# Layer 0 of a four-layer image network: attention with queries on the partitions instead of keys, and layer 2's row sums 1024 wide

## The chip, the cores and the metric

The kernel runs on one core of a Trainium2 chip. The metric is device time in microseconds (us) from start to end of one execution.

## The reference

The input x is four images (samples) of 128 channels by 64 x 64 = 4096 pixels, f32. Four layers follow each other; the change lies in layer 0 and in a small part of layer 2. Layer 0 for one sample:

```python
q = (q_w @ x + q_b).reshape(C, n)          # C = 128, n = 4096
v = (v_w @ x + v_b).reshape(C, n)
w, b = two small nets on q                 # (n,) each
norm   = sqrt(sum(q * q, axis=0))
k      = q / clip(norm, 1e-4)
logits = einsum('cn,cm->nm', k, q)         # keys n, queries m
mean   = mean(logits, axis=0)
sparse = relu(logits - mean * w[None, :] + b[None, :])
attn   = softmax(logits * sparse, axis=0)  # over the keys
attn   = clip(attn * (sparse != 0), 1e-8)
out    = einsum('cn,nm->cm', v, attn)
y = leaky(conv3x3(out) + lin_b) + x
```

Layer 1 is a state-space scan over the pixels of each sample (64 states), layer 2 a softmax attention whose logits are products of one number per row and one per column, and layer 3 two state-space scans over all samples.

## The kernel before

All samples pass layers 0 and 1 in turn: `layer0(b)`, `layer1(b)`, for b = 0 to 3. Layer 2 of sample b - 1 is worked off beside the layers of sample b: its row sums in `row_weights(b - 1)`, whose `beside(i)` is called once in each iteration of layer 0 (samples 1 to 3), and its products in `attend` beside layer 1. Layer 3 ends the kernel.

All instructions of the stages are recorded by a helper (line 111) that keeps program order on each engine. So each engine does its own instructions in the order in which the Python code issues them, and a wait holds up all that stands behind it on that engine. Nearly all groups in the profile therefore have the line L111 and are told apart by the names of their tiles.

`layer0` keeps keys on the partitions. A chunk c is 512 queries (`NCH` = 8 chunks). Iteration i of its loop takes one chunk's 512 queries and 256 keys: U = 16 iterations a chunk, S = 128 a sample. The steps of a tile of 128 x 2 x 512:

- `logits(i)`: two f32 matmuls into `lg` (PSUM, two buffers of two banks);
- `above(i)`, VectorE: t = lg + ncut, with the threshold `ncut` a 128 x 512 tile that repeats the row on all partitions;
- `weights(i)`, VectorE: e = max(t, 0) * lg;
- `shifted(i)`: GpSimd subtracts `bound` (an upper bound of the exponent per query), ScalarE takes Exp; every second t gets its sign from ScalarE;
- `sums(i)`, every second iteration: 32 columns of ones by e, in four column groups, add up `zs`, the sum of a query's weights over its keys;
- `masked(i)`: t becomes e where t > 0, on GpSimd and VectorE in turn;
- `floored(i)`, VectorE: the floor of 1e-8 times the sum, `fl`, which exists only when all keys of a chunk are done. So it runs LAG = 18 iterations behind;
- `product(i)`: two matmuls of values `vT` by t into `acc`, one iteration later.

`scales(c)` turns the sum into a floor and a factor 1/Z, `image(c)` multiplies `acc` by it into the padded image `ypad` (VectorE), and `convolved(c)` does the 3 x 3 convolution (nine matmuls), Prelu and residual. `thresholds(c)` makes `ncut` and `bound` for a chunk with four wide matmuls. These smaller steps wait in a queue; each iteration takes at most two of them and then one that starts with TensorE. The loop runs on for LAG + 2 iterations after the last logits, and there `first_tokens` (the first steps of layer 1) join in.

In sample 0 a loop ahead of this makes q, its norm and the keys k; for the others `tokens(b + 1)` in layer 1 does so and stores q, k and the norms (as rows) in DRAM.

`row_weights` gives ScalarE two activations of 512 columns an iteration (`junk`), each with a sum over its columns.

## Time and profile before

| | |
|---|---|
| three runs, median (lowest to highest) | 10499.42 us (10498.93 to 10503.0) |
| profiled execution, first to last instruction | 10494.9 us |
| busy in it: TensorE, VectorE, ScalarE, GpSimd | 8443.5, 9159.8, 6387.1, 8156.1 us |
| layer 0, sample 0: first logits to first scan of layer 1 | 59.3 to 786.0 us |
| the same, sample 1 | 1681.6 to 2423.8 us |
| layers 1 of the four samples | 786 to 1645, 2424 to 3307, 4085 to 4966, 5742 to 6610 us |
| last layer 2, then layer 3 | 6610 to 6950, 6950 to 10495 us |

The profile gives the span of the instructions alone; the median of the runs lies 4.5 us above it. Times of stages come from the first and last instruction of a kind in the trace. In the groups below a line reads: line, engine, operation, tile written and tiles read, shape, count, then busy time, mean length in ns of one, and the engine's idle time just before them with what ended it. The granted clock (PEclk) is TensorE's, as a share of full speed.

### The profile page before, as it was taken

Reading aid. Unit: us, or ns where it says so; the run is one execution under the profiler, and the core shown is the slowest. Engines: PE = TensorE matmul, PEld = TensorE weight load, DVE = VectorE, ACT = ScalarE, POOL = GpSimd, SP = SyncE. Lnnn points to the kernel's source line nnn. Section 1 sums busy time; section 2 is a strip of 40 time slices with the busy share of each in tenths; the row PEclk is TensorE's granted clock in tenths of the full one; section 3 lists DMA queues with packets and bytes.
Section 4 is the critical chain, followed back from the end, with each engine's and each line's share of the span. In section 5 each row is a group of like instructions: output and inputs, shape, how many; then the busy total and the mean of one; then the engine's idle time right before and its main releaser. Section 6 shows DMA issues by size and latency. Waiting matters only on the chain. (4 is left out here: it accounts for less than half of the span.)

```text
span 10494.9 us, 91078 instructions
## 1 busy us (share of the span) xinstructions
PE 8443.5 (80%) x28013; PEld 3021.6 (29%) x28088; DVE 9159.8 (87%) x6318; ACT 6387.1 (61%) x9576; POOL 8156.1 (78%) x3574
## 2 busy tenths in 40 slices
PE   8996667997887997887898887877777777777775
PEld 3331213332223333223333222322222222222221
DVE  7869998887998886999886999359999999999996
ACT  3334545666665665666665776456666666677765
POOL 6758896766887775888674888149999999989986
PEclk9997788998998999998999999888988989888886
DMA  1018882007885005887102888158888888888896
GB/s 37 12 37 201 194 194 85 18 14 189 211 203 149 15 14 129 201 213 191 33 16 63 206 211 200 32 133 199 207 198 206 204 202 208 215 223 224 228 227 176
DMA packets 512313, 1552.75 MB, mean 148 GB/s; under 512 B 84017, under 2 KB 91825, under 8 KB 511825
## 3 DMA queue, kind: packets, MB, share of 16 engines
q1 hardware_dynamic: 511824, 1546.92, 58.9%
q8 instruction: 223, 3.65, 0.2%
q14 instruction: 266, 2.17, 0.1%
HBM read 1349.40 MB, written 137.48 MB: 142 GB/s over the span
## 5 line engine op out<-in xcount | busy, mean ns | idle before, releaser
L111 POOL TENSOR_TENSOR p<-h,c_rep 128x1024 f32<-128x1024 f32 x2048 | 4807.9, 2359 | 734.8 <-DVE h L111 673.7
L111 DVE TENSOR_TENSOR_SCAN h<-da,carry,db 128x1024 f32<-128x1024 f32 x1536 | 3603.4, 2346 | 200.5 <-ACT da L111 17.8
L111 PE MATMUL db<-parts,sel 96*128 96x512 bf16 x4096 | 1401.5, 428 | 1460.3 <-DVE h L111 1408.2
L111 ACT ACTIVATE da<-row,A 128x1024 f32<-128x1024 f32 x1536 | 1761.1, 1147 | 359.4 <-DMA row<-d 341.0
L111 DVE TENSOR_TENSOR db<-b_rep,db 128x1024 f32<-128x1024 f32 x1536 | 1853.5, 1207 | 112.1 <-PE db L111 92.0
L111 POOL TENSOR_TENSOR e<-e,bound 128x1024 f32<-128x1024 f32 x512 | 1241.3, 2427 | 573.5 <-DVE e L111 573.0
L111 POOL TENSOR_TENSOR x<-row,b_rep 128x1024 f32<-128x1024 f32 x512 | 1208.8, 2361 | 123.8 <-DMA row<-d 122.8
L111 DVE TENSOR_TENSOR_SCAN h<-db,carry,x 128x1024 f32<-128x1024 f32 x512 | 1194.9, 2334 | 62.9 <-ACT db L111 35.3
L111 PE MATMUL total<-p,gather 128*32 128x512 f32 x8192 | 1225.7, 719 | 9.8 <-POOL p L111 9.8
L111 ACT ACTIVATE db<-db,A 128x1024 f32<-128x1024 f32 x512 | 555.3, 1085 | 1080.6 <-PE db L111 1026.5
L111 ACT ACTIVATE e<-e 128x1024 f32<-128x1024 f32 x512 | 540.9, 1057 | 1051.9 <-POOL e L111 1051.8
L111 PEld LDWEIGHTS <-sel 96*128 96x128 bf16 x4096 | 309.6, 101 | 3002.0 <-DVE h L111 2017.3
L111 PE MATMUL lg<-q,k 128*128 128x512 f32 x2048 | 1021.5, 623 | 106.5 <-DVE e L111 98.3
L111 PE MATMUL acc<-t,vT 128*128 128x512 f32 x2048 | 964.1, 595 | 3.3 <-DVE t L111 3.3
L111 PE MATMUL acc<-e,values 128*128 128x512 f32 x1536 | 854.9, 648 | 88.8 <-ACT e L111 62.9
L111 DVE TENSOR_TENSOR t<-lg,ncut 128x1024 f32<-128x1024 f32 x512 | 624.5, 1220 | 288.1 <-PE acc L111 264.0
L111 ACT ACT_TABLE_LOAD x617 | 791.6, 1283 | 38.8 <-DMA r<-y 12.3
L111 ACT ACTIVATE e<-gq,below,fcol 128x512 f32<-128x512 f32 x768 | 610.2, 805 | 87.0 <-PE acc L111 86.7
L111 POOL TENSOR_TENSOR t<-t,e 128x1024 f32<-128x1024 f32 x256 | 610.4, 2384 | 45.4 <-ACT t L111 45.4
L111 ACT ACTIVATE junk<-gp,ntop,fcol 128x512 f32<-128x512 f32 x768 | 619.5, 807 | 30.4 <-DMA gp<-g 17.7
L111 ACT COPY carry<-h 128x1 f32<-128x1 f32 x2048 | 373.5, 185 | 416.4 <-DVE h L111 411.4
L111 DVE SCALAR_TENSOR_TENSOR e<-t,lg 128x1024 f32<-128x1024 f32 x512 | 618.5, 1208 | 1.2
(259 smaller groups left out, 9927.5 us busy)
## 6 DMA issues: line engine op xcount, KB each, us to landing
row<-d SPq DMA_DIRECT2D x2048, 512.0 KB
parts<-split SPq DMA_DIRECT2D x912, 64.0 KB
b_rep<-bc SPq DMA_DIRECT2D x96, 512.0 KB
c_rep<-bc SPq DMA_DIRECT2D x96, 512.0 KB
d<-delta SPq DMA_DIRECT2D x76, 384.0 KB
r<-y SPq DMA_DIRECT2D x48, 512.0 KB
xq<-in_x SPq DMA_DIRECT2D x72, 256.0 KB
res<-x SPq DMA_DIRECT2D x32, 512.0 KB
```

What stands on the lines that cost most here:

```text
L111: return self.tc.keep_in_program_order(method(*args, **kwargs))
```

## The change

Queries go on the partitions. A tile is now 128 queries by 1024 keys; four tiles (J = 4) hold all keys of 128 queries, and a chunk still has U = 16 iterations.

- Threshold and bound are now one number per partition (`ncut`, `nbound`, 128 x 4 a chunk). `above` is a Relu with bias on ScalarE (all tiles of sample 0, every second of the others) or an add and max on VectorE. `weights` multiplies r by lg.
- Exp takes `nbound` as its bias and adds up its row (`accum_out`), so GpSimd's subtraction and the `sums`, `fl`, `zt`, `rz` matmuls go. `signs` makes r the mask on GpSimd (on ScalarE for odd tiles of sample 0); `masked` is on GpSimd for all tiles.
- `scaled(g)` makes `diag`, the identity times 1/Z, once for four tiles.
- `turned(i)`: eight 128 x 128 matmuls, weights e, moving operand `diag`, put the scaled weights back with keys on the partitions (`pt`, PSUM, one buffer). `floored` is a max with 1e-8 into `w`. `product` does eight matmuls of 128 columns. LAG is 6.
- `image` is a copy on ScalarE, and stands behind the next `product` in the loop.
- The norms stay in SBUF (`own`, 128 x 32), so the norm rows in DRAM and the steps that make them in layer 1's `tokens` go (`turned(u)`, `kept(u)` and a store there, other steps than the new `turned(i)`).
- `row_weights` has one activation of 1024 columns an iteration instead of two of 512.

```diff
-        LAG = U + 2
+        LAG = 6
...
+                def columns():
+                    held["th"] = misc("col_ps")[:, 0 : 3 * A].rearrange("p (a t) -> p t a", t=3)
+                    for a in range(A):
+                        m = bass.ts(a, P)
+                        pe.matmul(held["th"][:, 0:2, a], held["h"][:, m], self.w2, start=True, stop=True)
+                        pe.matmul(held["th"][:, 2:3, a], qs[c][:, m], kbar, start=True, stop=True)
...
+            def above(i, on_act):
+                if i < S and bool(b == 0 or i % 2 == 0) == on_act:
+                    c, a, j = at(i)
+                    r[i] = rp.tile([P, 2, NB], F32, name="r", tag="r")
+                    if on_act:
+                        act.activation(r[i], lg[i], AF.Relu, bias=ncut[c][:, a : a + 1])
+                    else:
+                        dve.tensor_scalar(flat(r[i]), flat(lg[i]), ncut[c][:, a : a + 1], 0.0, ALU.add, ALU.max)
+            def weights(i):
+                e[i] = ep.tile([P, 2 * NB], F32, name="e", tag="e")
+                dve.tensor_tensor(e[i], flat(r[i]), flat(lg.pop(i)), ALU.mult)
+            def exped(i):
...
+                act.activation(
+                    e[i], e[i], AF.Exp, bias=nbound[c][:, a : a + 1], accum_out=z[i // J][:, j : j + 1],
+                )
+                if b == 0 and i % 2:
+                    act.activation(r[i], r[i], AF.Sign)
+            def signs(i):
+                if b or i % 2 == 0:
+                    t = flat(r[i])
+                    pool.tensor_scalar(t, t, 0.0, None, ALU.is_gt)
+            def masked(i):
+                pool.tensor_tensor(e[i], e[i], flat(r.pop(i)), ALU.mult)
+            def turned(i):
+                pt[i] = turned_pair()
+                t = e.pop(i)
+                for m in range(N):
+                    pe.matmul(
+                        flat(pt[i])[:, bass.ts(m, P)], t[:, bass.ts(m, P)], diag[i // J], start=True, stop=True,
+                    )
+            def floored(i):
+                w[i] = wp.tile([P, N, P], F32, name="w", tag="w")
+                dve.tensor_scalar(flat(w[i]), flat(pt.pop(i)), 1e-8, None, ALU.max)
+            def product(i):
+                c, a, j = at(i)
+                if a == j == 0:
+                    acc[c] = ps1.tile([P, NB], F32, name="acc", tag="acc")
+                for m in range(N):
+                    pe.matmul(
+                        acc[c][:, bass.ts(a, P)], vT[:, N * j + m, :], w[i][:, m, :],
+                        start=(j == 0 and m == 0), stop=(j == J - 1 and m == N - 1),
+                    )
+            def image(c):
+                act.copy(ypad[...], acc.pop(c)...)
...
+                o = i - LAG
                 if i < S:
                     weights(i)
+                if 0 <= o < S:
+                    turned(o)
+                if 0 <= o - 1 < S:
+                    product(o - 1)
+                    if (o - 1) % U == U - 1:
+                        due[i + 1] = (o - 1) // U
                 if i + 2 < S:
                     logits(i + 2)
+                above(i + 1, True)
+                beside(i)
+                if i < S:
+                    exped(i)
+                    signs(i)
+                if 0 < i <= S:
+                    masked(i - 1)
+                    if i % J == 0:
+                        scaled(i // J - 1)
+                if 0 <= o < S:
+                    floored(o)
+                above(i + 1, False)
                 if i in due:
                     d = due.pop(i)
                     image(d)
```

## Prediction

> **What bounds the kernel now.** I read the page first: the chain of waits is empty here (it covers the last DMA alone), so the shares by engine are only an average over stages. I then split the span into stages. Layer 0 runs four times, from the start or from the last scan of layer 1 before it: 0 to 786, 1647 to 2424, 3310 to 4085 and 4969 to 5742 us. The rest the change hardly touches. The sum of engine times in single chunks of 512 queries (from one write of `ypad` to the next) comes next:

> ```profile
> core 0: us, PE busy (x) PEld busy (x) DVE busy (x) ACT busy (x) POOL busy (x), PEclk, DMA share, GB/s
> 393.13:473.40 80.27, 80.19 (x239) 31.70 (x238) 70.14 (x64) 27.38 (x30) 59.54 (x27) 1.00 0.05 14
> 2021.25:2103.74 82.49, 79.81 (x237) 31.23 (x236) 71.77 (x62) 54.45 (x93) 58.75 (x27) 1.00 0.05 16
> ```

> One chunk takes 80.3 us in sample 0 and 82.5 us in the others; TensorE is busy for 80.2 and 79.8 us of it at the full granted clock. VectorE's 71 us are close behind but below. What TensorE does there, in the groups of the second window:

> ```profile
> L111 PE MATMUL lg<-q,k 128*128 128x512 f32 x65 | 31.5, 605 | 2.0 <-DVE e L111 2.0
> L111 PE MATMUL acc<-t,vT 128*128 128x512 f32 x64 | 30.1, 592 | 0.0
> L111 DVE TENSOR_TENSOR t<-lg,ncut 128x1024 f32<-128x1024 f32 x16 | 19.5, 1221 | 10.7 <-PE acc L111 10.7
> L111 PE MATMUL conv_ps<-ypad,lin_wT 128*128 128x512 f32 x18 | 9.0, 609 | 0.0
> L111 PE MATMUL zs<-e,ones 128*32 128x512 f32 x64 | 8.5, 605 | 0.0
> ```

> TensorE waits 2 us in 82 for VectorE; VectorE waits 10.7 us for TensorE. A mean of 592 ns is a latency, since matmuls are pipelined; the price of one is the distance between starts. TensorE's timeline gives it (start, span, engine, operation, count):

> ```profile
> 1689.37 1.05 PE L111 MATMUL v_ps<-v_wT,xq 128*128 128x128 f32 x8
> 1690.26 1.02 PE L111 MATMUL lg<-q,k 128*128 128x512 f32 x2
> ...
> 2343.74 3.60 PE L111 MATMUL conv_ps<-ypad,lin_wT 128*128 128x512 f32 x8
> 2347.17 1.02 PE L111 MATMUL lg<-t,W_in 128*128 128x512 f32 x2
> ...
> 2354.04 1.84 PE L111 MATMUL lg<-mean_c,t 128*128 128x1 f32 x16
> 2355.74 2.82 PE L111 MATMUL acc<-t,vT 128*128 128x512 f32 x6
> ```

> Every matmul of the program is two instructions here (the two logits of an iteration and sample half stand as x4 and 64 a chunk). One with 512 moving columns costs (2347.17 - 2343.74)/8 = 0.429 us; one with 128 columns and weights of its own 0.89/8 = 0.111 us; one with a single column and new weights 1.70/16 = 0.106 us, so below 128 columns the weights set the price. Check on a chunk: 128 x 0.429 for `lg` and `acc` = 54.9; `zs`, four column groups at once, 64 in 7.9; convolution 18 x 0.429 = 7.7; thresholds 3.9; `fl`, `zt`, `rz` 2.8: 77.2, and 79.8 were busy. The accounting holds to 3%.

> **TensorE, part by part.** An iteration keeps its area (128 queries by 1024 keys for 256 keys by 512 queries), so `lg` stays at 4 x 0.429 = 1.72 us.
> - Removed: `zs` 7.9, `fl`, `zt`, `rz` 2.8, three of the four wide threshold matmuls (2.9) a chunk: 13.6 us.
> - Added: `turned`, 8 matmuls by `diag`, 16 instructions of 128 columns with 16 weight loads: 16 x 0.111 = 1.79 us an iteration, 28.5 us a chunk. The 16 small `columns` instructions, 16 x 0.106 = 1.7 us.
> - Dearer: `product` has the same columns, but 16 x 0.111 for 4 x 0.429: 28.5 instead of 27.5.

> After: 27.5 + 28.5 + 28.5 + 7.7 + 1.0 + 1.7 = 94.9 us, against 77.2 by the same accounting. No arrangement of the other engines gets below that.

> [...] The rows above say 111 and 429 for these f32 instructions, and I go by them.

> **The other engines, per iteration of at least 5.3 us.** VectorE: `weights` 1.21 (one operand in PSUM, as `e<-t,lg`), `floored` 1.21 (as `t<-t,fl`), `above` 1.21 every second time: 3.0. ScalarE: `above` as Relu, between 1.06 (`e<-e`) and 1.24 (the 1024 wide Identity with a bias); Exp with sum the same plus the 0.19 read of the accumulator; the row sum at 1024 wide: 0.81 at 512 and 3.80 at 4096 give 1.23, plus 0.19. In samples 1 to 3 that is 0.62 + 1.42 + 1.42 = 3.5; in sample 0 1.23 + 1.42 + half a Sign 0.52 = 3.2. GpSimd: `masked` 2.36 as now; `signs` has no row, it lies between 1.6 (eight times the 0.20 of a 128 wide memset) and 2.36 (a two-operand pass): at most 4.7. All are below 5.3, so none of it is paid, and neither is what the wider row sums save (2 x 0.99 - 1.42 = 0.6 us an iteration of ScalarE, already hidden behind TensorE). [...]

> **Waits.** `turned` waits for three engines, and `product` and `logits` stand behind it: `floored` of the iteration before ended some 2 us earlier, `diag` two iterations and `masked` five earlier. `logits` wait for `weights`, done early in the iteration. One wait is new and real: `acc` has one buffer, and `product` of a new chunk now stands ahead of `image`, which ScalarE does behind Relu, row sum and Exp: 1.23 + 1.42 + 1.42 + 0.6 = 4.7 us, less the 1.8 of `turned`. It costs 0 to 3.2 us at seven chunk ends; I take 2.3, as ScalarE starts a little ahead: about 97 us a chunk. Weight loads may also show after a wait: `lg` behind `zs` takes 1.82 instead of 1.72, so up to 0.1 at each of two places an iteration. I take 0, since after a full-width group (`acc` behind `lg`, 2020.87 to 2022.59) it is not seen.

> **Ends of the stage.** Now: first `lg` to first scan is 59.3 to 786.0 = 726.7 us in sample 0 and 1681.6 to 2423.8 = 742.1 in the others (sample 1). After:
> - the six iterations before the first `turned`: TensorE has 23 us of work (8 x 1.72 logits, seven values at 0.9, one threshold 2.7), the chain logits 1.9, Relu, `weights`, then Exp behind the row sum in one ScalarE queue, up to 6 an iteration, 36; taken 33, nearer the chain, since nothing else runs yet;
> - 122 iterations, 7.6 chunks of 97.2 = 741, less the 1.6 convolutions that come later (12): 729;
> - the tail: 13 passes of 1.79 = 23, convolutions 6 and 7 15.5, the first tokens 10.6 of TensorE, now beside 6 iterations instead of 18, waits between them some 10, and as now 18.4 us from the last convolution to the scan (2405.4 to 2423.8): 77.

> That is 839 for samples 1 to 3; sample 0, without row sums in ScalarE's queue, gets 3 less: +97 three times and +109. Ahead of it, sample 0 loses the 1x512 norm matmuls, roots and stores (eight chunks of 4.66 us; -5, between 0 and -8). In the others the `norms` load, `kbar_rep` and two wide matmuls go, but `values(0)` is waited for first: +2 each. The two `norms` steps leave layer 1's tokens, which run beside scans: 0. Sum: 291 + 109 + 1 = +401. The profiled execution spans 10,494.9 us, so 10,896; the median of the three runs lies 4.5 above that span: **10,900 us**.

> **Rivals.**
> 1. TensorE binds as above: 10,900, between 10,740 (no wait at `acc`, -64; the first six iterations and the tail at TensorE's work alone, -96) and 11,000 (0.1 us at two places of 512 iterations, +102). Chance 0.83.
> 2. GpSimd binds. The point is `signs` above 97.2/16 - 2.36 = 3.7 us. At 4.7 (twice a two-operand pass) iterations of samples 1 to 3 take 7.1: +1.0 x 128 x 3 = 384, 11,280; at 4.0, 11,010. For: no row. Against: no operation of that width here takes over 2.45 on average. Chance 0.08.
> 3. TensorE's gate: a granted clock of 0.9 instead of 1.0 in layer 0 adds a tenth to 4 x 777 us of TensorE work (eight chunks, values, tokens): 11,210. Layer 1 runs at 0.76 to 0.92, but with idle gaps; the busiest chunks of layer 0 are at 1.00. Chance 0.04.
> 4. Faster: short matmuls overlap better in long runs than in the bursts of 8 and 16 seen here. It decides at 0.09 us: 7.6 x (38 + 512 x 0.09) + 98 = 738, about the 742 of now. [...] Against it: even one column takes 0.106. Chance 0.03.
> 5. The change hides wholly, as if TensorE had been waiting: within 0.2%, 10,500. The 0.1 us of idle in sample 0's chunk speaks against it. Chance 0.02.

> The range of 10,740 to 11,070 is rival 1's own with the milder half of rival 2. Faster by over 0.2% (about what a measurement of this kernel can tell from no change) 0.03, same 0.02, slower 0.95.

> **What would show it.** Right: in layer 0 a chunk takes 96 to 99 us, TensorE busy all but 3 of them, `pt` and `acc` 256 instructions a chunk each with 0.111 between starts; VectorE under 55 us a chunk, GpSimd under 80, waits of `acc` for `ypad` once a chunk; layers 1 and 3 as long as before. Wrong: distances of the 128 wide matmuls under 0.09 or over 0.13; a TensorE wait for GpSimd's `e` in each iteration; a clock under 0.97 in layer 0; a tail over 100 us.

## The result, and the profile after

The changed kernel takes **11,022.1 us** (median of four runs, 11,020.6 to 11,024.6) against 10,499.3: **1.0497 times** as long, 95% interval 1.0482 to 1.0512. The forecast was 10,900 in a range of 10,740 to 11,070. Direction, mechanism and range held, the range in part by luck (see below); of the 523 us, 401 were foreseen.

TensorE binds, as forecast. The chunks of layer 0 after, in the same columns as before (two of sample 0, two of sample 1, each from one write of `ypad` to the next):

```profile
409.40:509.50 100.10, 98.06 (x612) 76.76 (x612) 38.91 (x43) 46.30 (x66) 61.17 (x28) 0.98 0.03 9
509.50:611.20 101.70, 99.71 (x612) 78.09 (x612) 38.87 (x43) 46.24 (x66) 61.16 (x28) 0.97 0.03 9
2062.30:2164.30 102.00, 99.72 (x612) 77.90 (x612) 49.16 (x51) 49.97 (x82) 83.13 (x37) 0.97 0.05 14
2164.30:2264.70 100.40, 98.10 (x612) 76.07 (x612) 49.17 (x51) 49.97 (x82) 83.18 (x37) 0.98 0.03 9
```

A chunk takes 100 to 102 us (80.3 and 82.5 before, 96 to 99 forecast); TensorE has 612 matmul instructions in it (239 before) and is idle for 2.0 to 2.3 us. In sample 1 VectorE fell from 72 to 49 us and GpSimd rose from 59 to 83 (under 80 forecast). The granted clock, 1.00 before, is now 0.97 to 0.98. The groups of the last of these chunks:

```profile
L111 POOL TENSOR_SCALAR r<-r 128x1024 f32<-128x1024 f32 x16 | 44.3, 2769 | 17.1 <-DVE e L111 14.5 <-DVE rz L111 2.5
L111 POOL TENSOR_TENSOR e<-e,r 128x1024 f32<-128x1024 f32 x17 | 40.1, 2361 | 0.0
L111 PE MATMUL acc<-w,vT 128*128 128x128 f32 x256 | 31.8, 278 | 2.3 <-ACT ypad L111 2.3
L111 PE MATMUL pt<-diag,e 128*128 128x128 f32 x256 | 31.3, 276 | 0.0
L111 PE MATMUL lg<-k,q 128*128 128x512 f32 x64 | 31.3, 613 | 0.0
```

`turned` (`pt`) and `product` (`acc`) have 256 instructions each, and the one wait in the chunk is the product's for `image`. TensorE's waits over four chunk ends (time in all, times, longest):

```profile
PE acc L111 <- ACT ypad L111: 9.2, 4, 2.3
```

That is 2.3 us each, the value taken. TensorE's timeline shows the prices:

```profile
2095.37 1.95 PE L111 MATMUL pt<-diag,e 128*128 128x128 f32 x16
2097.15 1.95 PE L111 MATMUL acc<-w,vT 128*128 128x128 f32 x16
2098.94 1.45 PE L111 MATMUL lg<-k,q 128*128 128x512 f32 x3
```

From one start to the next 16 instructions of 128 columns take 1.78 and 1.79 us: 0.111 each, as in the bursts of the kernel before.

Where the rest is, the stages of the trace show, against the same stages before. In sample 0 the first logits start at 80.7 us instead of 59.3 (forecast: 5 earlier). First logits to first scan takes 857.0, 860.1, 862.0 and 861.3 us, +130, +118, +121 and +120 (forecast +109 and +97 each). The three heads of samples 1 to 3 (last scan of the layer 1 before to first logits) take 6 us more together, the four layers 1 also 6, what follows them 4.

The start of sample 0, in the timelines of TensorE and of SyncE's queue:

```profile
56.74 0.51 PE L111 MATMUL col_ps<-kbar,q 128*128 128x1 f32 x2
78.85 2.04 PE L111 MATMUL v_ps<-v_wT,xq 128*128 128x128 f32 x8 [21.60 <-DMA xq<-in_x]
```
```profile
48.34 23.76 SPq L265 DMA_DIRECT2D A<-in_A_log x63
...
75.68 14.31 SPq L111 DMA_DIRECT2D xq<-in_x  x4
```

The values are now made ahead of the first logits, and their load of x stands on SyncE's queue behind 63 small loads of `A_log` for layer 1, which keep that queue for 23.8 us. TensorE waits 21.6 us.

The other part is the clock. Four neighbouring stretches of 3.41 us at a chunk end, in the columns of the chunk table:

```profile
2360.84:2364.25 3.41, 3.41 (x21) 2.45 (x21) 2.54 (x3) 0.95 (x1) 3.00 (x2) 1.00 0.00 0
2364.25:2367.67 3.42, 1.12 (x10) 0.93 (x9) 2.58 (x4) 3.42 (x7) 3.42 (x2) 1.00 0.00 0
2367.67:2371.08 3.41, 3.41 (x16) 3.22 (x16) 0.00 (x0) 2.22 (x5) 3.41 (x2) 0.50 0.00 0
2371.08:2374.49 3.41, 3.41 (x16) 2.04 (x15) 0.00 (x0) 0.00 (x0) 2.56 (x2) 1.00 0.00 0
```

In the second stretch TensorE waits 2.3 us for `image`; the third, whole and exactly, runs at half clock (0.50): the 128-column instructions that lie in it start 0.213 us apart, 0.112 at 1.00, so some 1.6 of its 3.41 us are lost. In this trace, and in that of the kernel before, the starts of all such stretches differ by multiples of 3.41333 us, to 0.01 us: they lie on a grid, and each stretch is called a cell of it below. Between the first turned matmul and the end of iteration 127 there are 8, 10, 11 and 11 half-clock cells in the four samples. Of the 40, 25 follow the wait at `acc` and 15 the run of `columns` (2.56 us of matmuls with one or two columns). The kernel before has two between the first write of `ypad` and the last logits of its four samples, both ahead of the second write.

### The profile page after: what moved, and what is told of

Same layout as the page of the kernel before. It is cut to its first block, busy times and chain, and to the rows that moved or that the text cites. A ratio compares the mean times of both kernels' runs of the same rounds, so it can differ in the third digit from the quotient of the medians.

```text
span 11022.8 us, 114821 instructions
## 1 busy us (share of the span) xinstructions
PE 9005.1 (82%) x40005; PEld 4497.3 (41%) x40080; DVE 8327.0 (76%) x5894; ACT 6428.3 (58%) x9524; POOL 8726.6 (79%) x3830
## 5 line engine op out<-in xcount | busy, mean ns | idle before, releaser
L111 POOL TENSOR_TENSOR p<-h,c_rep 128x1024 f32<-128x1024 f32 x2048 | 4806.2, 2358 | 745.5 <-DVE h L111 685.2
L111 DVE TENSOR_TENSOR_SCAN h<-da,carry,db 128x1024 f32<-128x1024 f32 x1536 | 3603.7, 2346 | 198.1 <-ACT da L111 13.7
L111 PE MATMUL db<-parts,sel 96*128 96x512 bf16 x4096 | 1400.2, 428 | 1497.5 <-DVE h L111 1408.9
L111 ACT ACTIVATE da<-row,A 128x1024 f32<-128x1024 f32 x1536 | 1761.2, 1148 | 346.3 <-DMA row<-d 342.3
L111 DVE TENSOR_TENSOR db<-b_rep,db 128x1024 f32<-128x1024 f32 x1536 | 1853.9, 1207 | 138.0 <-PE db L111 122.8
L111 DVE TENSOR_SCALAR w<-pt 128x1024 f32<-128x1024 f32 x512 | 627.0, 1225 | 1606.8 <-PE pt L111 1606.8
L111 POOL TENSOR_SCALAR r<-r 128x1024 f32<-128x1024 f32 x448 | 1240.5, 2769 | 661.6 <-DVE e L111 468.8
L111 PEld LDWEIGHTS <-sel 96*128 96x128 bf16 x4096 | 310.1, 101 | 3034.6 <-DVE h L111 2016.2
L111 POOL TENSOR_TENSOR x<-row,b_rep 128x1024 f32<-128x1024 f32 x512 | 1207.9, 2359 | 130.8 <-DMA row<-d 128.8
L111 DVE TENSOR_TENSOR_SCAN h<-db,carry,x 128x1024 f32<-128x1024 f32 x512 | 1194.8, 2334 | 68.2 <-ACT db L111 41.5
L111 PE MATMUL total<-p,gather 128*32 128x512 f32 x8192 | 1220.5, 711 | 18.8 <-POOL p L111 18.6
L111 POOL TENSOR_TENSOR e<-e,r 128x1024 f32<-128x1024 f32 x512 | 1206.5, 2361 | 13.7 <-issue 12.2
L111 ACT ACTIVATE db<-db,A 128x1024 f32<-128x1024 f32 x512 | 555.4, 1085 | 1107.8 <-PE db L111 1066.7
L111 ACT ACTIVATE r<-lg,ncut 128x1024 f32<-128x1024 f32 x320 | 356.6, 1114 | 1404.9 <-PE lg L111 1317.7
L111 PEld LDWEIGHTS pt<-diag,e 128*128 128x128 f32 x8192 | 1003.6, 194 | 232.7 <-issue 210.5
L111 PE MATMUL acc<-w,vT 128*128 128x128 f32 x8192 | 1038.1, 282 | 62.6 <-ACT ypad L111 62.6
L111 PEld LDWEIGHTS acc<-w,vT 128*128 128x128 f32 x8192 | 992.0, 198 | 67.9 <-ACT ypad L111 67.9
L111 PE MATMUL pt<-diag,e 128*128 128x128 f32 x8192 | 1017.4, 278 | 0.0
L111 PE MATMUL lg<-k,q 128*128 128x512 f32 x2048 | 995.0, 610 | 19.5 <-DVE e L111 19.5
L111 PE MATMUL acc<-e,values 128*128 128x512 f32 x1536 | 853.5, 647 | 90.1 <-ACT e L111 63.3
L111 ACT ACTIVATE e<-e,nbound 128x1024 f32<-128x1024 f32 x512 | 583.3, 1139 | 153.8 <-DVE e L111 153.5
```

What stands on the lines that cost most here:

```text
L111: return self.tc.keep_in_program_order(method(*args, **kwargs))
```

## The experiments

My theory after the result: TensorE's own work binds at the forecast prices, and the 122 us beyond the forecast are the load at the start, half-clock stretches, and longer first iterations. The rival left standing was GpSimd, whose `signs` took 2.77 us, above the bounds that I had set. Times below are ratios to the kernel before on the same chip; differences from the changed kernel (1.0497) are in its us, one thousandth being 10.5, and each carries some 15 to 20 us of uncertainty. Where that is too wide, the trace decides.

**GpSimd's compare left out** (`no_signs`):

```diff
-                if b or i % 2 == 0:
-                    t = flat(r[i])
-                    pool.tensor_scalar(t, t, 0.0, None, ALU.is_gt)
```

> The changed kernel without the compare on GpSimd: the mask there is r itself, so the weights are multiplied by r where r is above zero, not by 1 (this part of the computation is changed). GpSimd's busy time falls from 83 to about 39 us a chunk in samples 1 to 3. Theory (TensorE binds and GpSimd's 83 us lie wholly beside it): 11,022 within 0.3%. Rival (GpSimd's late masks delay the turned matmuls somewhere, at the chunk ends or in the first iterations): 50 us faster or more.

Measured 1.0495 [1.0481, 1.0510], -2 us. Two chunks:

```profile
2061.45:2163.36 101.91, 99.61 (x612) 78.31 (x612) 49.19 (x51) 49.99 (x81) 39.59 (x21) 0.97 0.05 14
2163.36:2265.35 101.99, 99.69 (x612) 78.29 (x612) 49.19 (x51) 49.99 (x81) 39.57 (x21) 0.97 0.03 9
```

GpSimd's 83 us became 40, and the chunk stayed at 102. Rival 2 falls: 44 us of compares a chunk cost nothing.

**Turned twice** (`double_turned`):

```diff
-                for m in range(N):
+                for m in [*range(N), *range(N)]:
                     pe.matmul(
                         flat(pt[i])[:, bass.ts(m, P)], t[:, bass.ts(m, P)], diag[i // J], start=True, stop=True,
```

> The changed kernel with every turned matmul done twice into the same place (the output is the same). Theory (TensorE binds layer 0, and one of these instructions costs 0.111 us): 16 x 0.111 = 1.78 us more in each of 512 iterations, 909 us more than the changed kernel, about 11,930; a chunk at 128 to 131 us. Rival 1 (GpSimd, busy 83 us a chunk of 100, is what sets the pace): TensorE would have 17 us of room a chunk, so at most 28.5 - 17 = 11.5 us a chunk more, 370 us. Rival 2 (long runs of short matmuls overlap better than the bursts did): below 0.09 us each, under 740 us more.

Measured 1.1284 [1.1263, 1.1304], +826. TensorE's timeline:

```profile
2304.43 3.73 PE L111 MATMUL pt<-diag,e 128*128 128x128 f32 x32
2308.00 1.95 PE L111 MATMUL acc<-w,vT 128*128 128x128 f32 x16
```

32 instructions in 3.57 us: 0.112 each in runs twice as long, so the short matmuls did not overlap better (rival 4). That is 914 us. The missing 88 are what the longer `turned` hides: ScalarE finishes `image` beside it, the wait at `acc` falls from 2.3 to 0.5 us (some 28 x 1.8 = 50), and no half-clock cell is left after these waits (15 in all instead of 40; 25 x 1.7 = 42). No run separated these two. TensorE paid here for each added instruction, 0.112 us.

**Image first** (`image_first`): the block moves to the top of the iteration.

```diff
                 o = i - LAG
+                if i in due:
+                    d = due.pop(i)
+                    image(d)
...
                 above(i + 1, False)
-                if i in due:
-                    d = due.pop(i)
-                    image(d)
...
```

> The changed kernel with one block moved: the copy of a finished chunk into the padded image is issued at the top of the iteration, ahead of the turned matmuls and of the product that reuses its accumulator. Theory 1 (the 2.3 us wait of the product at each of seven chunk ends a sample, and the half-clock window of 3.4 us that opens after that idle time, some 1.7 us of lost work): (2.3 + 1.7) x 28 = 112 us less than the changed kernel, about 10,910. Theory 2 (the half-clock windows have nothing to do with the idle time): 2.3 x 28 = 64 less, about 10,958, with as many half-clock windows as before. Theory 3 (the wait only moves, since ScalarE now does the copy ahead of Relu and TensorE then waits for that): no difference, 11,022, and a wait of the same length at another tile.

Measured 1.0389 [1.0374, 1.0403], -113. Between the first turned matmul and iteration 127 no wait at `acc` is left, and 3, 3, 1 and 2 half-clock cells instead of 8 to 11, all after `columns`. This part takes 711 to 714 us a sample instead of 739 to 746. That is theory 1, which gave 112; that it fits this closely is chance, given the uncertainty. The wait cost almost twice its length here, 113 / 28 = 4.0 us for 2.3.

**Columns in four steps** (`cols_spread`):

```diff
-                def columns():
...
-                    for a in range(A):
+                def columns(a):
+                    def go():
...
-                return [load, on_pe(first), hidden, on_pe(columns), mean, cut, top]
+                return [load, on_pe(first), hidden, *[columns(a) for a in range(A)], mean, cut, top]
```

> The changed kernel with the eight column matmuls of a chunk's thresholds (16 instructions of one or two columns in one run of 2.5 us) issued as four steps of two, in four different iterations. Theory (a run of 2.5 us of nearly empty matmuls opens half-clock windows, as idle time does, in about half of the chunks; each costs 1.7 us): about 4 x 4 x 1.7 = 27 us less than the changed kernel, 10,995, and windows only at the waits of the accumulator. Rival (those windows come from elsewhere and only fall there by chance): no difference over 5 us, as many windows.

Measured 1.0453 [1.0438, 1.0467], -46, more than the theory gave. The half-clock cells after `columns` are gone, but so are most of those after `acc`, though that wait is still there, 2.3 us long. The trace shows what differs. A wait of this kernel, in two neighbouring cells of its grid and the one after:

```profile
2151.87:2155.28 3.41, 2.54 (x18) 1.94 (x16) 2.05 (x3) 2.56 (x4) 2.11 (x1) 1.00 0.00 0
2155.28:2158.69 3.41, 1.98 (x17) 1.98 (x18) 1.75 (x4) 3.41 (x6) 3.32 (x4) 1.00 0.00 0
2158.69:2162.11 3.42, 3.42 (x16) 1.99 (x15) 0.00 (x0) 0.63 (x3) 3.34 (x4) 1.00 0.02 5
```

The wait is split, 0.87 us idle in one cell and 1.43 in the next, and the third stays at 1.00. I laid the waits at `acc` of all six kernels that keep them 2.0 to 2.8 us long on their grids (the changed kernel, this one, `no_signs`, `xv_early`, `decays_late`, `sums_512`), 168 in all. All 118 with 1.97 us or more of idle time in one cell are followed by a half-clock cell, none of the 46 with at most 1.89 us is, and of the four from 1.91 to 1.94 one is. In the changed kernel that makes 25 of 28, here 5 of 28. A chunk here takes 99.05 us in samples 1 to 3, 29.02 cells, so a wait that is split once is split again in the next chunk. That the two causes meet on one grid is read from the traces; no run shifted the grid alone.

**One load earlier** (`xv_early`, the first diff) and **that load with the decays late** (`decays_late`, both; `decay_loads` issues four of the 64 loads, `decay_signs` does their Exp and sign change):

```diff
+            vs = [values(c) for c in range(NCH)]
+            vs[0].pop(0)()
             queue.steps(1)
...
-            for c in range(NCH):
-                queue.add(values(c))
+            queue.add(*vs)
```
```diff
                 above(i + 1, False)
+                if b == 0 and 12 <= i < 12 + self.ins["A_log"].shape[1] // 4:
+                    self.decay_loads(i - 12)
+                if b == 0 and i == 48:
+                    self.decay_signs()
```

> The changed kernel with one load moved: the first 512 pixels of x for the values are loaded ahead of the weights of layers 1 and 2. Theory (in sample 0 that load stands behind 63 small loads on SyncE's queue, and the first logits behind the values): the first logits start at about 60 us instead of 80.7, so 21 us less than the changed kernel, about 11,001. Rival (the head of sample 0 is then held by something else, the queries' way through DRAM or the thresholds): 5 us less or nothing.

> The changed kernel with the first load of x for the values ahead of the weights of layers 1 and 2, and besides the 64 small loads of the decays issued four at a time in iterations 12 to 27 of sample 0, and their Exp and sign change at iteration 48. Theory (with the one load moved alone, the wait only went to VectorE's and ScalarE's queues, where these steps stand ahead of the first Relu and product and wait for the 64 loads: 11 us; and to the later loads of x): the first logits at 59 us instead of 80.7, the second without the 11 us, so 30 to 35 us less than the changed kernel, about 10,990. Rival (the head is then bound by the way of the queries through DRAM): 7 us less, as with the load alone.

`xv_early` measured 1.0490 [1.0475, 1.0504], -7, which by itself is within the uncertainty; the trace decides. Its first logits start at 58.7 us, 22 earlier, as the theory said, but the first scan only 10.6 earlier. VectorE's timeline shows where it went:

```profile
59.60 0.41 DVE L270 TENSOR_SCALAR A<-A 128x16 f32<-128x16 f32 x2
65.81 0.17 DVE L270 TENSOR_SCALAR A<-A 128x16 f32<-128x16 f32 x1 [5.80 <-DMA A<-in_A_log]
71.56 0.17 DVE L270 TENSOR_SCALAR A<-A 128x16 f32<-128x16 f32 x1 [5.58 <-ACT A L269]
72.56 1.22 DVE L111 TENSOR_TENSOR e<-r,lg 128x1024 f32<-128x1024 f32 x1 [0.83 <-ACT r L111]
```

The sign changes of the decays stand ahead of the first product on VectorE, and wait for the same 63 loads. `decays_late` takes them away: 1.0475 [1.0461, 1.0490], -23, the first logits at 59.7 us and the first scan 20.4 earlier, with the rest of the stage at its 857.6 us. The 30 to 35 that I expected were a miss: the 11 us behind the load alone are part of the 21, not on top of them.

**Row sums 512 wide again** (`sums_512`): `row_weights` of the kernel before, in the changed kernel.

> The changed kernel with layer 2's row sums again in two activations of 512 columns an iteration instead of one of 1024. Theory (TensorE binds, ScalarE has room): ScalarE's busy time rises from 50 to about 59 us a chunk of 100 in samples 1 to 3, and the time stays at 11,022 within 0.2%. Rival (ScalarE's queue delays Relu, so the product with the logits, so the buffers of the logits): up to 0.6 us in each of 384 iterations, 230 us more.

Measured 1.0501 [1.0487, 1.0516], +4, within the uncertainty: the 1024 wide row sums bring nothing that shows in the total. ScalarE's busy time in a chunk of sample 1 is 57.0 us instead of 50.0. In the trace this is the sum of two effects. The first is that the cover is not perfect: the wait for the copy that ScalarE makes is 2.8 us instead of 2.3 (seven chunk ends of sample 1):

```profile
PE acc L111 <- ACT ypad L111: 19.7, 7, 2.8
```

First logits to first scan takes 868.1, 866.6 and 870.9 us in samples 1 to 3, 5 to 10 more than in the changed kernel (sample 0, where the two do the same, takes 3.6 more). The second effect goes the other way: the heads of samples 1 to 3 take 30.7, 30.4 and 30.3 us, in the changed kernel 33.7, 36.6 and 37.1. There the first load for the wide row sums (`gp`) is issued ahead of those of q and k, and TensorE waits some 8 us for k:

```profile
1818.94 0.32 SPq L111 DMA_DIRECT2D gp<-g  x1
...
1819.81 5.18 SPq L111 DMA_DIRECT2D k<-k  x8
...
1824.85 1.94 PE L111 MATMUL th_ps<-q,w_T 128*64 128x512 f32 x2 [8.17 <-DMA k<-k]
```

With the narrow row sums that load stands behind them, and the wait for k is 5.6 us in sample 1 and gone in samples 2 and 3, where one of 4.3 to 4.4 us for `xq` is left.

**The three repairs together** (`four`), and **a transpose for the turning** (`transposed`), which has the repairs too (`diag` holds the column 1/Z there, `normed(o + 1)` stands in the loop behind `scaled`, and the signs of odd tiles are on ScalarE in all samples, not on GpSimd):

```diff
-                    pe.matmul(
-                        flat(pt[i])[:, bass.ts(m, P)], t[:, bass.ts(m, P)], diag[i // J], start=True, stop=True,
-                    )
+                    pe.transpose(flat(pt[i])[:, bass.ts(m, P)], t[:, bass.ts(m, P)], self.ident)
...
+            def normed(i):
+                dve.tensor_scalar(e[i], e[i], diag[i // J], None, ALU.mult)
...
-                if b == 0 and i % 2:
+                if i % 2:
                     act.activation(r[i], r[i], AF.Sign)
```

> The changed kernel with the three repairs together and the turned matmuls as they were: the image copied first (-112 alone), the columns in four steps (-45 alone), the decays' loads late (-24 alone). Theory 1 (half-clock windows come where TensorE is idle for most of one stretch of a fixed grid of 3.41 us, or in a long run of nearly empty matmuls; with neither left there is nothing that they could both save): the repairs overlap only in the windows that either of them takes away, so 181 less what is counted twice, about 20 to 30: 150 to 160 below the changed kernel, about 10,870 on the same scale. No half-clock window in a full chunk, a chunk at 96 us. The version with the transpose is then some 430 to 460 faster than this one (14.3 us in each of 32 chunks). Theory 2 (the repairs do not overlap): 181 below. Rival for the transpose (most of its gain came from elsewhere, as from the signs on ScalarE): this kernel under 300 slower than that one.

> A version made from all that was found: the image copied first, the column matmuls spread over four iterations, the decays' loads late, and the turning itself done by TensorE's transpose with the plain identity, with 1/Z multiplied into e by VectorE one iteration ahead (one pass of 1024 in SBUF more there); in samples 1 to 3 the signs of odd tiles are made by ScalarE, as in sample 0. Theory (TensorE binds; a transpose of f32 takes one instruction where the matmul takes two, at the same 0.111 us): 28.5 / 2 = 14.3 us a chunk less, so 32 x 14.3 = 457 below the other three steps together (about 11,022 - 112 - 45 - 33 = 10,832), 10,375, faster than the kernel before; a chunk at 81 to 83 us. Rival 1 (a transpose costs as much as the two instructions): 10,830. Rival 2 (VectorE's extra pass and GpSimd's masks hold each other up and one of them binds above 85 us a chunk): between 10,450 and 10,830.

`four` measured 1.0363 [1.0348, 1.0377], -141 for the 150 to 160 expected; `transposed` **0.9935 [0.9922, 0.9947]**, faster than the kernel before by 0.65%. That is some 10,430 us on the scale of the forecast, 56 above the 10,375 expected, mostly because that sum took 190 for the repairs, which together gave 141. A chunk of `four`, then one of `transposed`:

```profile
2101.20:2197.70 96.50, 96.50 (x615) 74.60 (x614) 49.11 (x51) 50.30 (x80) 83.22 (x37) 1.00 0.03 9
```
```profile
1948.47:2030.14 81.67, 81.67 (x485) 59.23 (x484) 74.61 (x68) 56.18 (x85) 64.23 (x29) 1.00 0.03 11
```

Both are TensorE from end to end at the full clock. In `four` the chunk lies 1.6 us above the 94.9 of the prediction's sum of TensorE's work. The transpose takes one instruction where the matmul takes two, in the timeline:

```profile
2112.74 1.04 PE L111 MATMUL pt<-ident,e 128*128 128x128 f32 x8
2113.62 1.95 PE L111 MATMUL acc<-w,vT 128*128 128x128 f32 x16
```

8 in 0.88 us, 14.8 us a chunk less. The two versions differ by 0.0428 or 449 us, the 430 to 460 expected; both rivals named with `transposed` and the one named with `four` fall. In `transposed` a chunk is then about as long as before the change (81.7 against 80.3 and 82.5), and it wins at the ends: from the last logits to the first scan 80 to 82 us, where the kernel before took 102 to 103, since 8 iterations follow the last logits and not 20.

## Why the prediction was right, and what it mis-sized

- **TensorE's work**: right. Instruction counts, 0.111 and 0.429 us, and who binds held; `double_turned` and `no_signs` show it from both sides, and `four` shows the sum bare: from the first turned matmul to iteration 127 it takes 711 to 712 us in every sample, and the forecast's 729 without its waits at `acc` is 711. Part of that is chance, since a full chunk of `four` is 1.6 us longer than the sum and the incomplete ones at the ends make up for it. Of the terms only `columns` was seen to be small: eight pairs 0.31 apart are 2.5 us, not 1.7. That the weights set the price below 128 columns was my inference from two rows (0.106 and 0.111), and no run showed it: an instruction of these pairs takes some 0.16.
- **The wait at `acc`**: 2.3 taken, 2.3 measured, in 21 of its 28 places (2.0 in sample 0).
- **The clock, taken as 1.00**: the largest miss. I priced a dip only as a whole stage at 0.9 (rival 3), against which a busy chunk at 1.00 spoke, and did not ask what a 2.3 us hole in a full TensorE does to the granted clock. 40 half-clock cells in the full iterations lose at most 1.7 us each, 68 us. From the first turned matmul to iteration 127 the trace has 743.7 to 745.5 us in samples 1 to 3 for the 729 of the sum, and 738.6 in sample 0.
- **The head of sample 0**: -5 forecast, +21 measured. The prediction knew that `values(0)` is now waited for, and priced it at 2 us in samples 1 to 3; in sample 0 I did not walk its load through SyncE's queue, past the 63 loads. `decays_late` gives the 21 back; the 5 us less do not show (59.7 against 59.3 before).
- **The first six iterations**: 33 taken (30 in sample 0), 39 to 40 measured in each sample, beyond the upper end of 36. That is 28 us in all. The changed kernel shows half-clock cells there too, two a sample; what the other microseconds are was not tested, and the cause stays open.
- **The tail**: 77 forecast, 76.9 to 77.3 measured in samples 1 to 3, 79.1 in sample 0.
- **The heads of samples 1 to 3**: +6 in all, as forecast, but not for its reasons. In `sums_512` they are 2.5 to 3.6 us shorter than in the kernel before. So the parts that the forecast added up to +2 each give about -3, and the wide row sums, which it did not count there and whose first load stands ahead of q and k, make up the rest. That the sum fits is luck.
- **`signs`**: 2.77 us, above the 1.6 to 2.36 of my bounds, and below the 3.7 from which GpSimd decides. The ends were wrong, the margin covered it.
- **The range**: 11,022 lies in it in part by luck. Its upper end was made of weight loads after waits and of half of GpSimd's rival; neither came, and the clock, the head and the first iterations filled the room.

In the profiled execution 528 us were added: 401 forecast, 26 at the head, 89 in the four stages (28 in the first iterations, some 57 net from the first turned matmul to iteration 127, mostly the clock, the rest tail and rounding), 6 in layer 1, 4 behind it, 2 by rounding.

## What to carry to other kernels

When one engine is busy to the last microsecond, as TensorE was here, price the change by its instructions times their start-to-start distance (94.9 us a chunk by that sum, 96.5 measured in `four`). What another engine saved beside it was worth nothing here (without 44 us of compares a chunk, -2 us in all); look instead for a form of the same step with fewer instructions, as the transpose was here (14.8 us a chunk). On such a TensorE price a short wait above its length: 2.3 us cost up to 4 here, by where the wait fell on the clock's grid, and moving the step that it waited for cost nothing. When a step begins to be waited for, walk its load through every queue that it stands in; taking one instruction out of a jam may only show the next queue with the same jam (in `xv_early` the first logits came 22 us earlier, the first scan 10.6), and a load that is moved forward may hold back those behind it (with that of the row sums ahead, TensorE waits some 8 us for k).
